# A four-layer graph network on one core: own terms two blocks ahead, a held bank of sums, later scatters and more buffers in layer 1

## The chip, the cores and the metric

The kernel runs on one core of one Trainium2 chip. Its metric is the device time of one execution in microseconds (us). TensorE (PE) multiplies matrices, VectorE (DVE) and ScalarE (ACT) work elementwise, GpSimd (POOL) here issues indirect DMAs (gathers and scatters by a list of row numbers), and SyncE (SP) issues the plain DMAs. [...]

## The reference, cut to what matters

Four layers follow each other; each adds its result to `x` (2708 rows of 128 numbers) and normalises every row. `adj` is a 2708 x 2708 matrix with about 0.6% of its entries set.

```python
x = _layernorm(x + _L0_gnn_ref(x, adj), axis=-1)            # adj.T @ x, divided by the column sums
x = _layernorm(x + _L1_gnn_ref(x, adj, msg_w, ...), axis=-1)
x = _layernorm(x + _L2_gnn_ref(x, adj, W, ...), axis=-1)    # adj @ (x @ W), batch norm, leaky relu
x = _layernorm(x + _L3_gnn_ref(x, adj, w1, ...), axis=-1)   # attention over neighbours, 4 heads

# layer 1, which the change is about
s = node_feats @ msg_w[:, :D].T
d = node_feats @ msg_w[:, D:].T
messages = jax.nn.gelu(s[:, None, :] + d[None, :, :] + msg_b, approximate=False)
aggregated = jnp.einsum('ijd,ij->id', messages, adj)
combined = jnp.concatenate([node_feats, aggregated], axis=-1)
new_feats = combined @ upd_w.T + upd_b
h = jax.nn.gelu(new_feats, approximate=False) + node_feats
mu, var = jnp.mean(h, axis=-1, keepdims=True), jnp.var(h, axis=-1, keepdims=True)
return (h - mu) / jnp.sqrt(var + LN_EPS) * ln_w + ln_b
```

Only the nonzero entries of `adj` contribute to `aggregated`. So for each row `i` the kernel needs the row `d[j]` of each neighbour `j`, adds the row's own term `s[i]` (with the bias), takes the gelu and sums with the weights `adj[i, j]`.

## The kernel before, in words

Rows are handled in 22 blocks of 128 (the last has 20). During layer 0, while the rows of `adj` stream through nine buffers, VectorE finds the nonzero entries of each row (`extract`) and the rows are ranked by their number of neighbours, in two groups of 13 and 9 blocks. Rows are then scattered to memory in that order (`dx_dram` holds for each row its `d` and its `x`, `d_dram` holds `d` in the original order), so that the rows of one block have about equally many neighbours: `CAPS` gives the number of gathers of each block, from 30 to 8, 368 in all.

Layer 1 goes over the blocks in the order `TURNS`; one pass of that loop is called a turn here. In a turn:

- `own_row` (L821) loads the next block's `d` and `x` on SP into `x_s` (three buffers).
- `messages` takes the one bank of the PSUM pool `own_ps`. It transposes the block's `x` (L832, TensorE), copies it out (L833, ScalarE), multiplies by the message weights and adds the bias (L834, L835), which leaves `s` in that bank. VectorE adds `s` to the block's own `d` (L849), ScalarE takes the gelu (L850). Then for each chunk of up to 8 neighbours POOL issues one gather per neighbour into a `msg` tile (L245; five tiles), VectorE adds `s` to all of them (L858), ScalarE takes the gelu (L861), and VectorE multiplies each by its weight and accumulates into one of two sums in the same bank (L844, L846), the last two into `parts`.
- In some turns `spread` prepares index lists of layer 3: lists loaded by SP (L580) are multiplied by a mask on VectorE (L601), multiplied on TensorE into free columns of the same bank (L607) and copied out (L614, L615).
- One or two other blocks of `adj` are transposed beside this (`transposed`, L931 on TensorE, L936 on ScalarE) and stored to `at_dram` by SP (L938); nine blocks are still searched by `extract`.
- `update` takes the one bank of `tail_ps`: it adds and transposes `parts` (L872), copies (L879), multiplies (L881 to L883), takes the gelu (L888), adds the residual (L889), normalises twice on VectorE (`x_n`, L319), scatters the result to `x2_dram` on POOL (L253), transposes it (L899, L901) and multiplies it by layer 2's weights (L903), and ScalarE puts the product into `xw` (L904).
- From the twelfth turn on `layer2` gathers whole rows of the transposed matrix (one indirect DMA each) and adds 22 products per block into six PSUM banks (L957).

The order of instructions on each engine is not the order of the source in this part. The pools record dependences, and a scheduler fixes one order for each engine ahead of time, by priority in the order of the source and by its own estimate of times[...]. Buffers of a pool are reused once the last reader is done. Layers 0 and 3 have orders written out by hand for some engines. After layer 1 the kernel loads `x2_dram`, does the batch norm of layer 2, and layer 3 gathers rows of 644 numbers 400 times.

Of the kernel before, what the change touches and what calls it, by code (L numbers as in the profile page):

```python
# [9 lines left out]
FP = mybir.dt.float32  # L10
AF = mybir.ActivationFunctionType
ALU = mybir.AluOpType
# [3 lines left out]
P = 128  # L16
N = 2708
D = 128
# [63 lines left out]
GOT = 9  # L82


@with_exitstack
def gnn_resnorm_kernel(
# [248 lines left out]
    with ExitStack() as layer:  # L335
# [6 lines left out]
        sums_ps = part.enter_context(tc.tile_pool(name="sums_ps", bufs=7, space=PSUM))  # L342
        hand.enter_context(tc.manual_schedule(engines={engine.DVE}))
# [26 lines left out]
        def weight(src, name):  # L370
            raw = small.tile([P, P], FP, name="raw_w")
            nc.sync.dma_start(raw, src)
            pt = own_ps.tile([P, 512], FP, name="pt_w", tag="own")
            nc.tensor.transpose(pt[:, 0:P], raw, ident)
            t = work.tile([P, P], FP, name=name)
            nc.scalar.copy(t, pt[:, 0:P])
            return t
# [101 lines left out]
        def ranking(g):  # L479
# [17 lines left out]
            key_row = work.tile([P, SPLIT, P], FP, name="key_row")  # L497
# [314 lines left out]
        msgs = layer.enter_context(tc.tile_pool(name="msgs", bufs=5))  # L812
# [5 lines left out]
        def own_row(b):  # L818
            n = BLOCKS[b][1]
            x_s = mine.tile([P, 2, D], FP, name="x_s", bufs=3)  # L820
            nc.sync.dma_start(  # L821
                x_s[0:n],
                dx_dram[b * P : b * P + n, :].rearrange("p (t d) -> p t d", t=2),
            )
            return x_s

        def messages(b, x_s, three):
            n, kk = BLOCKS[b][1], CAPS[b]
            po = own_ps.tile([P, 512], FP, name="own", tag="own")
            x_st, s_ps = mine.tile([P, P], FP, name="x_st"), po[:, P : 2 * P]  # L830
            acc = (po[:, 0:P], po[:, 3 * P : 4 * P])
            nc.tensor.transpose(po[:, 0:n], x_s[0:n, 1, :], ident[0:n, 0:n])  # L832
            nc.scalar.copy(x_st[:, 0:n], po[:, 0:n])  # L833
            nc.tensor.matmul(s_ps[0:n], lhsT=x_st[:, 0:n], rhs=ws_t, start=True, stop=False)  # L834
            nc.tensor.matmul(  # L835
                s_ps[0:n], lhsT=ones[0:1, 0:n], rhs=msgb[0:1, :], start=False, stop=True
            )
# [11 lines left out]
            nc.vector.tensor_tensor(mk, mk, s_ps[0:n], ALU.add)  # L849
            nc.scalar.activation(mk, mk, AF.Gelu)  # L850
            weigh(0, mk)
            for c0, c1 in chunks_of(kk):
                kc = c1 - c0
                msg = msgs.tile([P, 8, D], FP, name="msg")
                for k in range(kc):
# [3 lines left out]
                    mk, mk, s_ps[0:n].unsqueeze(1).to_broadcast((n, kc, D)), ALU.add  # L859
# [4 lines left out]
            for i, b3 in enumerate(three):  # L864
                spread(b3, po, 256 + 64 * i)
            return x_st, parts

        def update(b, x_s, x_st, parts):
# [16 lines left out]
            x_n = mine.tile([P, 1, D], FP, name="x_n")  # L885
# [12 lines left out]
            scatter(x2_dram, perm[0:n, b : b + 1], x_n[0:n, 0, :])  # L898
# [5 lines left out]
            nc.scalar.copy(xw[0:n, b, :], px)  # L904

        def transposed(b, rows, cleared=False):
# [10 lines left out]
            for j0 in range(0, NBLK, 4):  # L917
                count = min(4, NBLK - j0)
                pt = bank.tile([P, 4, P], FP, name="pt_a", tag="bank")
                at = small.tile([P, 4, P], FP, name="at_sb", bufs=3)  # L920
# [51 lines left out]
        ahead = own_row(0)  # L972
        left = list(range(SPLIT, NBLK))
        for i, b in enumerate(TURNS):
            if i == SPLIT - 2:
                sorted_lists(1)
            x_s, ahead = ahead, own_row(TURNS[i + 1]) if i + 1 < NBLK else None
# [6 lines left out]
            x_st, agg = messages(b, x_s, three)  # L984
            for _ in range(2 if i < 1 else 1):
                if left:
                    e = left.pop(0)
                    transposed(e, rows_of[e], True)
                    run(extract(e, rows_of[e]))
                    if e == NBLK - 3:  # L990
                        run(place(SPLIT, NBLK - 2, lists(SPLIT, NBLK - 2)))
                    if e == NBLK - 1:
                        run(place(NBLK - 2, NBLK, lists(NBLK - 2, NBLK)))
            update(b, x_s, x_st, agg)
# [7 lines left out]
            if i >= 11:  # L1002
                for k in range(2 * (i - 11), min(i, 2 * (i - 10))):
                    layer2(k)
        layer2(NBLK - 1)
# [1026 lines left out]
```

## Time and profile before

| | |
|---|---|
| time, median of 3 runs | 1605.33 us (1604.46 to 1609.47) |
| time of the profiled execution | 1957.99 us |
| its span, first to last instruction | 1956.3 us |
| mean granted TensorE clock in it | 0.668 |
| busy over the span: PE, DVE, ACT, POOL | 1248.6, 1173.2, 768.6, 896.4 us |
| first and last gather of messages | 229.8 and 1013.4 us |
| first and last scatter of layer 1's results | 352.4 and 1044.5 us |

The profile is one execution, recorded by hardware. A row of its groups gives a source line, an engine, an operation and its tiles (written tile, arrow, read tiles; numbers of buffers are left out, so `x_dram<-x_n` is the scatter into `x2_dram`), the count, then busy time and mean duration, then the engine's idle time just before these instructions and what ended it. "issue" is idle time in which the engine waited for nothing that the profile shows; "remote" is idle time ended by none of the core's engines or known transfers. A row of the timeline gives start, duration, the instruction, and in brackets the idle time before it. The profiled execution took 352.7 us more than the median of the timed ones, so its times are to be read with that in mind.

### The profile page before, as it was taken

The numbers are of one execution on the slowest core, as the hardware profiler recorded it, in microseconds if no ns is written. First come the engines' busy times: TensorE is split into PE (matmuls) and PEld (weight loads), VectorE is DVE, ScalarE is ACT, GpSimd is POOL, SyncE is SP. The second block draws the span as 40 slices with busy tenths as digits, with TensorE's granted clock in tenths as the row PEclk, the third lists the DMA queues.
The fourth block names the chain that finished last, engine by engine and source line by source line (L and its number), as shares of the span: only waits on it lengthen the run. The fifth ranks groups of instructions, "written<-read, shape, count | busy, mean of one in ns | idle before, by whom it ended". The sixth has DMA issues, their size and how long they took to land. (4 is left out here: it accounts for less than half of the span.)

```text
span 1956.3 us, 23628 instructions
## 1 busy us (share of the span) xinstructions
PE 1248.6 (64%) x5771; PEld 866.9 (44%) x5771; DVE 1173.2 (60%) x4900; ACT 768.6 (39%) x3134; POOL 896.4 (46%) x996
## 2 busy tenths in 40 slices
PE   7972414443345564556585647888798888877884
PEld 7972313333234453445465313445444444444444
DVE  8999536763353533343346626677678777676773
ACT  3475424542222311111111414455455555455543
POOL 1002655555544445444430454555565556555430
PEclk9985655555555576666677755677677777677675
DMA  8541547765444624332331474766475665756530
GB/s 288 228 160 41 170 94 195 202 169 145 125 90 117 173 96 96 109 132 88 141 110 37 153 222 130 190 189 194 140 206 178 173 178 153 189 159 191 153 109 7
DMA packets 164926, 289.61 MB, mean 148 GB/s; under 512 B 46850, under 2 KB 118752, under 8 KB 157679
## 3 DMA queue, kind: packets, MB, share of 16 engines
q0 software_dynamic: 60496, 190.76, 34.4%
q1 hardware_dynamic: 96739, 92.56, 15.6%
q10 hardware_dynamic: 7544, 4.69, 0.9%
q8 instruction: 48, 0.79, 0.2%
q14 instruction: 99, 0.81, 0.1%
HBM read 242.50 MB, written 45.35 MB: 147 GB/s over the span
## 5 line engine op out<-in xcount | busy, mean ns | idle before, releaser
L245 POOL DMA_INDIRECT g<-t_dram,idx x400 | 402.2, 1005 | 310.8 <-issue 169.2
L245 POOL DMA_INDIRECT msg<-d_dram,idx x368 | 348.7, 947 | 272.1 <-issue 225.7
L1324 ACT ACTIVATE sum_junk<-g 126x128 bf16<-126x128 f32 (+3 forms) x1024 | 302.6, 298 | 142.3 <-issue 60.8
L1293 PE MATMUL z<-x,copies 32*126 32x512 f32 (+3 forms) x800 | 220.3, 917 | 60.7 <-DVE g L1490 33.9
L957 PE MATMUL acc<-x_nat,at_rows 128*128 128x128 f32 (+2 forms) x968 | 168.8, 335 | 64.5 <-issue 52.6
L931 PE MATMUL pt_a<-ident,rows 128*128 128x128 f32 (+2 forms) x475 | 119.0, 408 | 131.5 <-ACT at_sb L936 106.9
L1490 DVE TENSOR_TENSOR g<-g,z 126x1536 f32<-126x1536 f32 (+3 forms) x100 | 175.1, 1751 | 40.1 <-remote 25.4
L1324 ACT ACTIVATION_READ_ACCUMULATOR sum_junk<-g 126x1 f32 (+3 forms) x1024 | 193.5, 189 | 0.0
L957 PEld LDWEIGHTS acc<-x_nat,at_rows 128*128 128x128 f32 (+2 forms) x968 | 151.2, 240 | 78.8 <-issue 67.5
L1298 PE MATMUL z<-g,ident 126*126 126x512 f32 (+3 forms) x200 | 168.5, 937 | 0.1
L1370 PE MATMUL po_s<-wm,g 126*128 126x24 f32 (+6 forms) x800 | 124.7, 310 | 59.7 <-DVE wm L1357 53.8
L931 PEld LDWEIGHTS pt_a<-ident,rows 128*128 128x128 f32 (+2 forms) x475 | 86.4, 212 | 154.8 <-ACT at_sb L936 120.9
L1370 PEld LDWEIGHTS po_s<-wm,g 126*128 126x128 f32 (+3 forms) x800 | 120.8, 237 | 75.1 <-DVE wm L1357 63.8
L1316 DVE SCALAR_TENSOR_TENSOR g<-g,a_ps 126x1536 f32<-126x1536 f32 (+6 forms) x100 | 151.1, 1511 | 0.0
L406 PE MATMUL acc<-x_nat,rows 128*128 128x129 f32 (+3 forms) x1012 | 128.5, 288 | 25.9 <-DMA rows<-in_adj_dram 15.1
L406 PEld LDWEIGHTS acc<-x_nat,rows 128*128 128x128 f32 (+2 forms) x1012 | 122.9, 197 | 31.1 <-DMA rows<-in_adj_dram 16.1
L846 DVE SCALAR_TENSOR_TENSOR own<-msg,ls,own 128x128 f32<-128x128 f32 (+1 forms) x302 | 106.5, 353 | 37.4 <-remote 13.5
L1293 PEld LDWEIGHTS z<-x,copies 32*126 32x126 f32 (+3 forms) x800 | 65.3, 250 | 97.9 <-issue 54.2
L1308 DVE SCALAR_TENSOR_TENSOR g<-z,a 126x128 f32<-126x128 f32 (+3 forms) x400 | 92.0, 287 | 19.4 <-DMA g<-t_dram,idx 9.4
L431 DVE FIND_INDEX8 ci<-cv,rows 128x8 uint32<-128x247 f32 (+2 forms) x242 | 101.6, 420 | 0.0
L436 DVE MAX8 cv<-rows 128x8 f32<-128x247 f32 (+2 forms) x242 | 98.0, 411 | 2.2 <-POOL rows L396 2.2
L1298 PEld LDWEIGHTS z<-g,ident 126*126 126x126 f32 (+3 forms) x200 | 41.7, 261 | 122.1 <-issue 109.1
(293 smaller groups left out, 2084.0 us busy)
## 6 DMA issues: line engine op xcount, KB each, us to landing
rows<-in_adj_dram SPq DMA_DIRECT2D x34, 1354.0 KB
at_dram<-at_sb SPq DMA_DIRECT2D x105, 256.0 KB
g<-t_dram,idx POOLq DMA_INDIRECT x400
msg<-d_dram,idx POOLq DMA_INDIRECT x368
t_dram<-t_row SPq DMA_DIRECT2D x21, 256.0 KB
x_s<-dx_dram SPq DMA_DIRECT2D x21, 128.0 KB
at_dram<-at_sb SPq DMA_DIRECT2D x21, 64.0 KB
d_dram<-dx SPq DMA_DIRECT2D x5, 256.0 KB
```

Of the source, the lines that this page charges most:

```text
L245: nc.gpsimd.indirect_dma_start(out=dst, out_offset=None, in_=table[0:N, :], in_offset=bass.IndirectOffsetOnAxis(ap=index, axis=0),)
L406: nc.tensor.matmul(accs0[k][0:m, c0 : c0 + f1 - f0], lhsT=rows[0:n, j0 : j0 + m], rhs=x_nat[0:n, b, f0:f1], start=k not in started, stop=( ...
L431: nc.vector.max_index(out=ci[0:n, at], in_max=cv[0:n, at], in_values=rows[0:n, c0 : c0 + cw])
L846: nc.vector.scalar_tensor_tensor(to, m, v, last, ALU.mult, ALU.add)
L931: nc.tensor.transpose(pt[0:m, j, 0:n], rows[0:n, c0 : c0 + m], ident[0:n, 0:n])
L957: nc.tensor.matmul(accs2[ib // 4][0:m, (ib % 4) * D : (ib % 4 + 1) * D], lhsT=at[0:n, i0 : i0 + m], rhs=xw[0:n, b, :], start=(k == 0 and i ...
L1293: nc.tensor.matmul(z3[0:e, r, :] if r < 3 else z1[0:e], lhsT=copies[g][rows, j, :], rhs=own[b][1][rows, :], start=True, stop=r < 3, skip_g ...
L1298: nc.tensor.matmul(z1[0:e], lhsT=ident[0:e, 0:e], rhs=g4[0:e, 3, 0:HD], start=False, stop=True, skip_group_check=True,)
L1316: nc.vector.scalar_tensor_tensor(z, z, 0.0, a_ps[0:e].unsqueeze(1).to_broadcast((e, count, HD)), ALU.max, ALU.mult)
L1324: nc.scalar.activation(junk[0:e], g4[0:e, r, hd * D : (hd + 1) * D], AF.Identity, accum_out=sc[0:e, r, hd : hd + 1],)
L1370: nc.tensor.matmul(po[:, p0 * HEADS : (p0 + g) * HEADS], lhsT=g4s[i][0:e, r, HD : HD + D], rhs=wm[0:e, 4 * i + r, :, :], start=True, stop= ...
L1490: nc.vector.tensor_tensor(z, z, z3[0:e], ALU.add)
```

## The change

Four things change in layer 1, and two tiles move to another pool.

1. **Own terms.** A new function `own_terms` makes the transposed `x` and `s` for a block; `s` is copied to SBUF. It uses the bank of `tail_ps` (same tag as the update's tile) and is called for the first two blocks before the loop and then in turn `i` for the block of turn `i + 2`, ahead of `update`. `own_row` is called three turns ahead instead of one. The adds in `messages` read `s` from SBUF.
2. **Sums.** One bank, `sums1`, is taken once before the loop and holds the two running sums in all turns; `spread` alternates between two sets of columns of it.
3. **Results.** `update` appends `x_n` to a list; `put_results` scatters what is in the list after the next turn's `messages`, and once after the loop.
4. **Buffers.** `msg` 5 to 6 tiles, `x_s` 3 to 4, `x_st` 2 to 3 and a new `s` with 3, `x_n` 2 to 3, the transposed tiles `at_sb` 3 to 5.
5. `raw_w` and `key_row` come from a pool `head`, which is given back at the end of layer 0.

```diff
+MSGS = 6
...
+        head = part.enter_context(tc.tile_pool(name="head", bufs=1))
...
-            raw = small.tile([P, P], FP, name="raw_w")
+            raw = head.tile([P, P], FP, name="raw_w", bufs=2)
...
-            key_row = work.tile([P, SPLIT, P], FP, name="key_row")
+            key_row = head.tile([P, SPLIT, P], FP, name="key_row")
...
-        msgs = layer.enter_context(tc.tile_pool(name="msgs", bufs=5))
+        msgs = layer.enter_context(tc.tile_pool(name="msgs", bufs=MSGS))
...
-            x_s = mine.tile([P, 2, D], FP, name="x_s", bufs=3)
+            x_s = mine.tile([P, 2, D], FP, name="x_s", bufs=4)
...
-        def messages(b, x_s, three):
+        def own_terms(b, x_s):
+
+            n = BLOCKS[b][1]
+            tp = tail_ps.tile([P, 512], FP, name="terms", tag="tail")
+            x_st = mine.tile([P, P], FP, name="x_st", bufs=3)
+            s = mine.tile([P, D], FP, name="s", bufs=3)
+            nc.tensor.transpose(tp[:, 0:n], x_s[0:n, 1, :], ident[0:n, 0:n])
+            nc.scalar.copy(x_st[:, 0:n], tp[:, 0:n])
+            pn = tp[0:n, P : 2 * P]
+            nc.tensor.matmul(pn, lhsT=x_st[:, 0:n], rhs=ws_t, start=True, stop=False)
+            nc.tensor.matmul(pn, lhsT=ones[0:1, 0:n], rhs=msgb[0:1, :], start=False, stop=True)
+            nc.scalar.copy(s[0:n], pn)
+            return x_s, x_st, s
+
+        def messages(b, x_s, s, three, spreads):
             n, kk = BLOCKS[b][1], CAPS[b]
-            po = own_ps.tile([P, 512], FP, name="own", tag="own")
-            x_st, s_ps = mine.tile([P, P], FP, name="x_st"), po[:, P : 2 * P]
-            acc = (po[:, 0:P], po[:, 3 * P : 4 * P])
-            nc.tensor.transpose(po[:, 0:n], x_s[0:n, 1, :], ident[0:n, 0:n])
-            nc.scalar.copy(x_st[:, 0:n], po[:, 0:n])
-            nc.tensor.matmul(s_ps[0:n], lhsT=x_st[:, 0:n], rhs=ws_t, start=True, stop=False)
-            nc.tensor.matmul(
-                s_ps[0:n], lhsT=ones[0:1, 0:n], rhs=msgb[0:1, :], start=False, stop=True
-            )
+            acc = (sums1[:, 0:P], sums1[:, 3 * P : 4 * P])
...
-            nc.vector.tensor_tensor(mk, mk, s_ps[0:n], ALU.add)
+            nc.vector.tensor_tensor(mk, mk, s[0:n], ALU.add)
...
-                    mk, mk, s_ps[0:n].unsqueeze(1).to_broadcast((n, kc, D)), ALU.add
+                    mk, mk, s[0:n].unsqueeze(1).to_broadcast((n, kc, D)), ALU.add
...
-                spread(b3, po, 256 + 64 * i)
-            return x_st, parts
+                spread(b3, sums1, P + 128 * (spreads % 2) + 64 * i)
+            return parts
...
-            x_n = mine.tile([P, 1, D], FP, name="x_n")
+            x_n = mine.tile([P, 1, D], FP, name="x_n", bufs=3)
...
-            scatter(x2_dram, perm[0:n, b : b + 1], x_n[0:n, 0, :])
+            results.append((b, x_n))
...
+        results = []
+
+        def put_results():
+            while results:
+                b, x_n = results.pop(0)
+                n = BLOCKS[b][1]
+                scatter(x2_dram, perm[0:n, b : b + 1], x_n[0:n, 0, :])
...
-                at = small.tile([P, 4, P], FP, name="at_sb", bufs=3)
+                at = small.tile([P, 4, P], FP, name="at_sb", bufs=5)
...
-        ahead = own_row(0)
+        sums1 = own_ps.tile([P, 512], FP, name="sums1", tag="own")
+        rows1 = [own_row(b) for b in TURNS[:3]]
+        terms = [own_terms(b, rows1.pop(0)) for b in TURNS[:2]]
...
-            x_s, ahead = ahead, own_row(TURNS[i + 1]) if i + 1 < NBLK else None
+            x_s, x_st, s = terms.pop(0)
+            if i + 3 < NBLK:
+                rows1.append(own_row(TURNS[i + 3]))
...
-            x_st, agg = messages(b, x_s, three)
+            agg = messages(b, x_s, s, three, i)
+            put_results()
...
+            if rows1:
+                terms.append(own_terms(TURNS[i + 2], rows1.pop(0)))
             update(b, x_s, x_st, agg)
...
+        put_results()
         layer2(NBLK - 1)
```

## The prediction

> **What bounds the kernel now.** I read four views in this order: the stretches, POOL's groups, VectorE's groups, then the timeline where engines stand still. Layer 1, with the re-read of the adjacency matrix and layer 2's sums beside it, runs from about 230 to 1050 us of the profiled span. First view: time, then each engine's busy time with its instruction count, granted clock, DMA share and GB/s.
>
> ```profile
> core 0: us, PE busy (x) PEld busy (x) DVE busy (x) ACT busy (x) POOL busy (x), PEclk, DMA share, GB/s
> 0.00:230.00 230.00, 150.01 (x1118) 139.42 (x1118) 205.54 (x1119) 121.02 (x190) 44.34 (x114) 0.83 0.50 172
> 230.00:1050.00 820.00, 402.23 (x1916) 329.54 (x1915) 362.67 (x1652) 213.92 (x472) 400.05 (x421) 0.60 0.46 129
> 1050.00:1130.00 80.00, 49.86 (x226) 32.36 (x225) 53.40 (x230) 30.67 (x87) 25.81 (x38) 0.81 0.37 118
> 1130.00:1956.00 826.00, 646.46 (x2516) 365.54 (x2516) 551.55 (x1901) 402.97 (x2386) 426.17 (x424) 0.68 0.58 163
> ```
>
> No engine is half busy in those 820 us. POOL issues 421 indirect DMAs there. The groups of POOL in that stretch (busy, mean ns, idle before and what ended it):
>
> ```profile
> L245 POOL DMA_INDIRECT msg<-d_dram,idx x368 | 348.7, 947 | 272.1 <-issue 225.7 <-ACT at_sb L936 30.3 <-ACT back L916 10.3
> L253 POOL DMA_INDIRECT x_dram<-x_n,perm x22 | 21.9, 996 | 134.1 <-DVE own L846 65.2 <-DVE x_n L319 51.7 <-DVE spread L601 14.2
> L245 POOL DMA_INDIRECT at_rows<-at_dram,perm x22 | 20.8, 946 | 6.7 <-issue 6.4 <-remote 0.3
> L253 POOL DMA_INDIRECT lists_dram<-lists,rank x9 | 8.9, 988 | 5.4 <-DMA lists_dram<-lists,rank 3.2 <-issue 2.1
> ```
>
> In the timeline consecutive gathers lie 1.25 us apart: 0.95 busy and 0.30 of gap. So 421 of them need 400 + 421 x 0.30 = 526 us without any wait. The other 820 - 526 = 294 us are waits: about 131 at scatters of results that wait for x_n, the rest for a free message buffer. VectorE's groups in the same stretch:
>
> ```profile
> L858 DVE TENSOR_TENSOR msg<-msg,own 128x896 f32<-128x896 f32 (+4 forms) x55 | 57.4, 1044 | 2.7 <-DVE rs_t L273 1.2 <-DVE rs_u L283 0.6
> ...
> L601 DVE TENSOR_TENSOR spread<-lists,of_row 128x126 f32<-128x126 f32 (+3 forms) x48 | 13.8, 291 | 104.3 <-remote 58.5 <-PE own L607 19.6 <-PE pt_a L931 13.1
> ...
> L889 DVE SCALAR_TENSOR_TENSOR new<-new,x_s 128x128 f32<-128x128 f32 (+1 forms) x22 | 6.4, 290 | 112.3 <-ACT new L888 95.2 <-issue 16.9
> L849 DVE TENSOR_TENSOR x_s<-x_s,own 128x128 f32<-128x128 f32 (+1 forms) x22 | 6.3, 286 | 49.5 <-PE own L835 36.8 <-remote 9.2 <-PE pt_a L931 3.5
> ```
>
> The first row is the one to weigh: the add that takes the gathered rows waited 2.7 us in all. In this execution the gathers were never late; VectorE was held by the update (L889), the own terms (L849) and the spreads. But the execution is not the timed one: its own time is 1957.99 us (span 1956.3), the median 1605.33, 352.7 less. The timeline of VectorE shows what is extra:
>
> ```profile
> 718.97 0.15 DVE L281 TENSOR_SCALAR rs_u<-rs_t 128x1 f32<-128x1 f32 x1 [0.61 <-issue]
> 721.07 0.16 DVE L283 TENSOR_TENSOR rs_u<-rs_u,rs_t 128x1 f32<-128x1 f32 x1 [1.95 <-remote]
> 722.46 0.16 DVE L285 SCALAR_TENSOR_TENSOR rs_y<-rs_u,rs_y 128x1 f32<-128x1 f32 x1 [1.23 <-DVE rs_u L283]
> 723.16 0.22 DVE L273 SCALAR_TENSOR_TENSOR rs_t<-rs_y,ln_var 128x1 f32<-128x1 f32 x1 [0.55 <-DVE rs_y L285]
> 724.56 0.15 DVE L289 TENSOR_SCALAR rs_t<-rs_t 128x1 f32<-128x1 f32 x1 [1.18 <-DVE rs_t L273]
> ```
>
> A chain of VectorE alone, 0.15 us a step, stops for 0.6 to 2 us between steps; from 768 to 806 us TensorE issues single matmuls 2 to 3 us apart in the same way, also with nothing to wait for. I take such stalls for the cost of recording. VectorE's waits that "issue" or "remote" ended sum to 5, 201, 6 and 104 us in the four stretches; sharing 352.7 us by 201/316 gives layer 1 some 224 us of it, so an estimated 596 us in a timed run. POOL's 526 us are then 88% of the stage, and 70 us of POOL waits are left. That is the bound I work with.
>
> [...]947 ns of POOL for each gather, whatever the other engines do. [...]here gathers queue behind a waiting scatter (13.67 us at 756 us). [...]
>
> **The change part by part**, with the built order of both kernels.
>
> Results scattered later. The same 22 scatters move behind gathers: the first 20 stood on average 16.2 gathers behind the last gather of the next block, now 29.2; the tightest, of the thirteenth turn, goes from 0 to 25, those of turns 16 to 18 from 7 or 8 to 16, 14 and 9. The last two stay at 0. One clean turn (809.2 to 828.1 us in the trace) has x_n 1.6 us after the turn's last add, so 5 us of lead or 4 gathers suffice once compute keeps up. Of the 70 us I leave 25 to the stretch behind the last gather (37 us in the profile, 1013 to 1050), which stays; the other 45 split as 131 : 163, so 20 us at scatters. I take 18 as removed. x_n's third buffer costs nothing while VectorE does not reach the fourth result before the first has gone.
>
> Message buffers, 5 to 6. Look-ahead goes from 5 x 6.7 = 33 gathers (42 us) to 40 (50 us). It cuts a stall by at most 8 us. Of the 25 us of buffer waits I take 8; bounds 0 and 25.
>
> Own terms ahead. Per block 1 transpose, 2 fp32 matmuls and a copy move; one copy of s is new (22 x 0.27 = 6 us of ScalarE, hidden: it is busy 214 of 820). VectorE's 49.5 us before L849 go, worth nothing on a POOL-bound stage except as slack. Reading s from SBUF: no gain, since 128x128 adds take 286 ns with PSUM (L849) and 282 without (L877). Two transposed copies and own-row buffers more: nothing by themselves. The terms now use the tail bank, between the last copy of one update and the first matmul of the next. Chain from the clean turn: x_n to the last copy 1.6 us, terms 2.5 (0.27 + 0.27 + 1.35 + 0.27 and hops), update to L889 2.8: 6.9 us, where VectorE has S, two adds and a multiply (2.8 us) ahead of L889. Uncovered: 4 us per turn. A clean turn takes 18.9 us, POOL needs (20 + 3) x 1.25 = 28.8 for that block: covered there. In the last four turns POOL needs 14 to 21 us and cover is gone: 4 x 1 us = 4 us lost.
>
> Own rows loaded three ahead. The 22 loads on SP stay, each now waiting for the previous turn's L889 instead of the one before that; behind them queue stores of transposed tiles and list loads for the spreads, 156.8 us of such SP waits today. List loads are issued two turns early. Bounds: 0 and 10 us lost through spreads; I take 0. One bank held: a spread's matmuls now stand among later sums in places (15 waits of VectorE for TensorE on the last sums, before none), under 1 us each and covered. Order of the neighbour search on VectorE: its work is the same and moves behind messages; 0. Memory for the key row freed early: 0.
>
> Sum: 18 + 8 - 4 = 22 us of the timed stage. Against the profiled execution it is 1957.99 - 22 or more, as its waits are larger; against the median, 1605.33 - 22 = 1583.
>
> **Rivals.** A: the timed run has cheaper gathers than 1.25 us, so the chain TensorE, ScalarE, VectorE is the bound, as in the trace. For: gathers never late there. Against: the stalls are the recording's. Then L849's 49.5 us and part of L889's 112 go: 60 to 75 us, 1530 to 1545. B: POOL is already dense, or its buffer waits were only the recording's: nothing moves, 1600 to 1610. C, slower: the tail bank. If every hop of the serial chain queues behind two layer-2 products (4 passes of 0.176 us, that is 165.8 us over 944 records of L957; five gaps: 3.5 us), the chain is 10.4 us and 7.6 uncovered, so a turn of 18.9 becomes some 25 us; POOL needs less than that in the last six turns (14 to 25), which lose 4 to 8 us each: about 35, less 15 of gain kept before: 1625. It decides once a turn's chain is longer than its gathers. For: before, the bank is already taken from 927.0 to 956.1 us of a 31.7 us turn. Against: most of that is x_n waiting in VectorE's order.
>
> **How the numbers follow.** Forecast 0.42 (own range 1565 to 1598), A 0.20, B 0.12, C 0.26. Faster 0.62, same 0.12, slower 0.26; 0.3%, or 5 us, is what this measurement can tell from no change. The range 1542 to 1625 leaves about a tenth outside at each end, in A and in C.
>
> **What would show it.** In the profile after: scatters of x_n without idle time of POOL before them (131 us now); L849's wait near zero; gathers dense at 1.25 us with fewer buffer waits; L889's wait no larger than 112. Wrong if L889 or the first matmul of the update waits more, with POOL idle for message buffers in the last turns (C), or if POOL's waits shrink and the time does not (B).

## The result: 2.8% slower, and where the profile shows it

The kernel after takes 1650.35 us (median of 4 runs, 1648.64 to 1656.08), the kernel before beside it 1607.40 us: a ratio of 1.0281, 95% interval 1.0252 to 1.0310. The forecast was 1583, its range ended at 1625.

Executions fall into two groups, whatever the kernel: before takes 1605 to 1614 us in the faster group and 1937 to 1952 us in the slower one (the expectations speak of two kinds of chip, but chip number 6 is on record with both, so that the chip decides is not shown).

The times above are from the faster group. The profile of before that the prediction read, 1957.99 us, is from the slower one, so its extra time was not a cost of recording: the profile of a copy of before with the same instruction lists (the first experiment) was recorded in the same way and took 1609.49 us, beside a median of 1609.96. VectorE's waits ended by "issue" or "remote" sum to 0.0 us in its layer 1, where the prediction summed 201. This copy is the profile of before in what follows.

The stretches of the copy of before in the faster group (time, busy time of each engine, TensorE clock, DMA share, GB/s); layer 1 is 223 to 830 us, batch norm up to 896, layer 3 behind:

```profile
core 0: us, PE busy (x) PEld busy (x) DVE busy (x) ACT busy (x) POOL busy (x), PEclk, DMA share, GB/s
223.00:830.00 607.00, 346.11 (x1886) 289.85 (x1885) 354.34 (x1632) 213.41 (x469) 402.26 (x423) 0.67 0.62 174
830.00:896.00 66.00, 43.53 (x224) 31.04 (x224) 52.16 (x223) 28.17 (x82) 24.10 (x37) 0.82 0.38 118
896.00:1607.00 711.00, 619.32 (x2541) 351.23 (x2539) 550.09 (x1909) 400.97 (x2392) 426.60 (x426) 0.72 0.70 192
```

The same stretches of after:

```profile
223.00:869.00 646.00, 349.19 (x1882) 295.67 (x1880) 335.33 (x1630) 215.84 (x488) 410.65 (x423) 0.65 0.56 163
869.00:935.00 66.00, 43.55 (x229) 30.46 (x228) 52.48 (x225) 28.83 (x84) 24.66 (x38) 0.84 0.40 124
935.00:1648.00 713.00, 613.45 (x2534) 348.63 (x2533) 550.45 (x1906) 400.88 (x2391) 425.77 (x425) 0.73 0.68 191
```

Layer 1 goes from 607 to 646 us, all else stays within 2 us. With 423 gaps of 0.30 us POOL is taken for 402 + 127 = 529 of the 607 us before and 538 of the 646 after; its waits grow from 78 to 108 us. POOL's groups in layer 1 (busy, mean ns | idle before), first of the copy of before:

```profile
L245 POOL DMA_INDIRECT msg<-d_dram,idx x368 | 348.8, 948 | 136.2 <-issue 107.0 <-ACT at_sb L937 13.3 <-DMA msg<-d_dram,idx 6.7
L253 POOL DMA_INDIRECT x_dram<-x_n,perm x22 | 21.9, 997 | 55.3 <-DVE x_n L319 33.6 <-DVE own L847 16.4 <-issue 3.1
...
L253 POOL DMA_INDIRECT lists_dram<-lists,rank x9 | 8.9, 985 | 6.2 <-DMA lists_dram<-lists,rank 2.8 <-DVE own L847 1.6 <-issue 1.5
```

then of after:

```profile
L247 POOL DMA_INDIRECT msg<-d_dram,idx x368 | 358.4, 974 | 120.8 <-issue 100.4 <-DMA msg<-d_dram,idx 10.3 <-ACT x_st L837 2.2
L255 POOL DMA_INDIRECT x_dram<-x_n,perm x22 | 21.9, 995 | 82.0 <-DVE x_n L321 46.8 <-DVE spread L604 19.9 <-DVE sums L855 12.0
...
L255 POOL DMA_INDIRECT lists_dram<-lists,rank x9 | 8.8, 973 | 25.6 <-DVE rs_t L275 10.7 <-DVE ln_var L293 7.4 <-DMA lists_dram<-lists,rank 4.4
```

Four numbers move: waits at the scatters of results 55.3 to 82.0 (+26.7), waits at the scatters of layer 3's lists 6.2 to 25.6 (+19.4), the gathers themselves 348.8 to 358.4 (+9.6), waits before gathers 136.2 to 120.8 (-15.4). They sum to 40.3 us; the two spans differ by 40.9, the medians by 43. (Each gather has at least 0.30 us of idle time before it, 110 us for 368 of them, in both profiles.)

VectorE's groups say the same from its side. The copy of before (add of messages; update's first add after the gelu; own add):

```profile
L859 DVE TENSOR_TENSOR msg<-msg,own 128x896 f32<-128x896 f32 (+4 forms) x55 | 57.4, 1044 | 15.8 <-DMA msg<-d_dram,idx 14.9 <-DVE ln_var L306 0.2
L890 DVE SCALAR_TENSOR_TENSOR new<-new,x_s 128x128 f32<-128x128 f32 (+1 forms) x22 | 6.4, 291 | 63.5 <-ACT new L889 63.5
L850 DVE TENSOR_TENSOR x_s<-x_s,own 128x128 f32<-128x128 f32 (+1 forms) x22 | 6.3, 286 | 21.8 <-PE own L836 21.7
```

and after:

```profile
L867 DVE TENSOR_TENSOR msg<-msg,s 128x896 f32<-128x896 f32 (+4 forms) x55 | 57.7, 1050 | 139.8 <-DMA msg<-d_dram,idx 121.2 <-issue 18.4
...
L858 DVE TENSOR_TENSOR x_s<-x_s,s 128x128 f32<-128x128 f32 (+1 forms) x22 | 6.4, 290 | 30.3 <-ACT s L841 30.3
L898 DVE SCALAR_TENSOR_TENSOR new<-new,x_s 128x128 f32<-128x128 f32 (+1 forms) x22 | 6.4, 289 | 43.8 <-ACT new L897 43.7
```

VectorE now waits 139.8 us before it adds to gathered rows (121.2 of them ended by the rows landing), 15.8 before, while POOL waits for VectorE. Each waits for the other in turn. One such turn in the timeline of after, VectorE first (start, duration, instruction, idle before):

```profile
697.22 0.96 DVE L867 TENSOR_TENSOR msg<-msg,s 128x768 f32<-128x768 f32 x1 [3.48 <-DMA msg<-d_dram,idx]
698.09 0.21 DVE L275 SCALAR_TENSOR_TENSOR rs_t<-rs_y,ln_var 128x1 f32<-128x1 f32 x1
...
700.13 0.15 DVE L291 TENSOR_SCALAR rs_t<-rs_t 128x1 f32<-128x1 f32 x1
705.24 0.96 DVE L867 TENSOR_TENSOR msg<-msg,s 128x768 f32<-128x768 f32 x1 [4.96 <-DMA msg<-d_dram,idx]
706.11 0.15 DVE L293 TENSOR_TENSOR ln_var<-rs_y,rs_t 128x1 f32<-128x1 f32 x1
...
711.98 0.34 DVE L321 TENSOR_SCALAR x_n<-new,sums,ln_var 128x128 f32<-128x128 f32 x1
```

and POOL in the same microseconds:

```profile
702.16 0.94 POOL L247 DMA_INDIRECT msg<-d_dram,idx  x1 [0.30 <-issue]
...
704.65 0.94 POOL L247 DMA_INDIRECT at_rows<-at_dram,perm  x1 [0.30 <-issue]
712.60 1.00 POOL L255 DMA_INDIRECT x_dram<-x_n,perm  x1 [7.01 <-DVE spread L604]
713.91 0.97 POOL L247 DMA_INDIRECT msg<-d_dram,idx  x1 [0.30 <-issue]
```

The rsqrt steps of one block's normalisation (L275 to L293) are threaded between the message adds of the next block. At 700.13 they stop: the next instruction of VectorE is an add whose rows land at 705.24. Only then does the chain go on, through a second normalisation threaded between the sums of those rows, to x_n at 711.98, and POOL, which came to that scatter at 705.6, stands 7 us. The gathers of the block after next start only at 713.91. The last releaser named is a spread, but x_n is ready at 712.32.

The built order is the order of each engine's instructions in the program as it was built. In the records above both engines keep to theirs: VectorE's chain stands 5.0 us behind that add, the next gather behind a scatter that waits 7.0 us. Counted in the built order, x_n of a block stood behind the adds of 12.9 gathers beyond its own block on average before, and 27.3 after. What matters at its scatter is the lead, the number of gathers that POOL issues between the last one that x_n needs and the scatter: from the thirteenth turn on 15, 16, 14, 13, 8, 7, 11, 5, 6, 0 before and 5, 2, 0, 0, 0, 1, 0, 0, 0, 0 after. The scatters of turns 14 to 19 wait 5.4, 7.0, 5.4, 3.6, 7.5 and 5.9 us there; in the copy of before all but two of turns 12 to 19 wait 0.3 (the others 1.6 and 0.8). The copy of before waits elsewhere: 48 of its 55.3 us stand at the eleventh scatter (16.9) and the last three (31.1; 32.7 in after).

### The profile page after: what moved, and what is told of

Same layout as the page of the kernel before. It is cut to its first block, busy times and chain, and to the rows that moved or that the text cites. A ratio compares the mean times of both kernels' runs of the same rounds, so it can differ in the third digit from the quotient of the medians.

```text
span 1648.7 us, 23658 instructions
## 1 busy us (share of the span) xinstructions
PE 1160.0 (70%) x5771; PEld 818.3 (50%) x5771; DVE 1147.3 (70%) x4900; ACT 768.3 (47%) x3156; POOL 904.3 (55%) x996
## 5 line engine op out<-in xcount | busy, mean ns | idle before, releaser
L247 POOL DMA_INDIRECT msg<-d_dram,idx x368 | 358.4, 974 | 120.8 <-issue 100.4
L1318 PE MATMUL z<-x,copies 32*126 32x512 f32 (+3 forms) x800 | 208.9, 875 | 23.0 <-DVE g L1515 21.5
L974 PE MATMUL acc<-x_nat,at_rows 128*128 128x128 f32 (+2 forms) x968 | 156.0, 318 | 85.7 <-DMA at_rows<-at_dram,perm 75.6
L948 PE MATMUL pt_a<-ident,rows 128*128 128x128 f32 (+2 forms) x475 | 102.8, 375 | 145.0 <-ACT at_sb L953 132.0
L974 PEld LDWEIGHTS acc<-x_nat,at_rows 128*128 128x128 f32 (+2 forms) x968 | 138.8, 223 | 96.3 <-DMA at_rows<-at_dram,perm 78.7
L1323 PE MATMUL z<-g,ident 126*126 126x512 f32 (+3 forms) x200 | 162.5, 906 | 10.3 <-DMA g<-t_dram,idx 10.2
L867 DVE TENSOR_TENSOR msg<-msg,s 128x896 f32<-128x896 f32 (+4 forms) x55 | 57.7, 1050 | 139.8 <-DMA msg<-d_dram,idx 121.2
L1395 PE MATMUL po_s<-wm,g 126*128 126x24 f32 (+6 forms) x800 | 114.9, 296 | 31.0 <-DVE wm L1382 29.1
L1395 PEld LDWEIGHTS po_s<-wm,g 126*128 126x128 f32 (+3 forms) x800 | 111.3, 220 | 46.7 <-DVE wm L1382 41.1
L870 ACT ACTIVATE msg<-msg 128x896 f32<-128x896 f32 (+4 forms) x55 | 50.1, 915 | 169.8 <-DVE msg L867 149.9
L855 DVE SCALAR_TENSOR_TENSOR sums<-msg,ls,sums 128x128 f32<-128x128 f32 (+1 forms) x302 | 105.1, 348 | 0.9 <-ACT msg L870 0.2
L1333 DVE SCALAR_TENSOR_TENSOR g<-z,a 126x128 f32<-126x128 f32 (+3 forms) x400 | 91.8, 285 | 12.8 <-PE z L1323 12.1
```

Of the source, the lines that this page charges most:

```text
L247: nc.gpsimd.indirect_dma_start(out=dst, out_offset=None, in_=table[0:N, :], in_offset=bass.IndirectOffsetOnAxis(ap=index, axis=0),)
L855: nc.vector.scalar_tensor_tensor(to, m, v, last, ALU.mult, ALU.add)
L948: nc.tensor.transpose(pt[0:m, j, 0:n], rows[0:n, c0 : c0 + m], ident[0:n, 0:n])
L974: nc.tensor.matmul(accs2[ib // 4][0:m, (ib % 4) * D : (ib % 4 + 1) * D], lhsT=at[0:n, i0 : i0 + m], rhs=xw[0:n, b, :], start=(k == 0 and i ...
L1318: nc.tensor.matmul(z3[0:e, r, :] if r < 3 else z1[0:e], lhsT=copies[g][rows, j, :], rhs=own[b][1][rows, :], start=True, stop=r < 3, skip_g ...
L1323: nc.tensor.matmul(z1[0:e], lhsT=ident[0:e, 0:e], rhs=g4[0:e, 3, 0:HD], start=False, stop=True, skip_group_check=True,)
```

## The experiments

All theories are named in the expectations: D, VectorE's order just shown; C, the serial chain through the tail bank (the slower rival of the prediction); S, the later search and list loads. In those texts the "turns 13 to 18" of the search-first kernel and the "turns 12, 14 and 16" of the one with s from SBUF count from zero; they are turns 14 to 19 and turns 13, 15 and 17 here.

Two parts can be judged without a run. With the scatter put back into `update`, or with `sums1` taken anew in each turn, the instruction lists of all five engines are those of after, instruction for instruction. So "results later" and "one bank held" are in the source only; what moved the scatters was the scheduler, by what else changed: by the prediction's own count, more buffers alone move them from 16.2 to 27.1 gathers behind.

**Copy of before** (only the pool `head`; the instruction lists are those of before).

> Kernel before with only the move of raw_w and key_row to the pool head. The instruction lists of all five engines are the same as before. Every theory: 1607 us, within 0.3%. It is run for its profile: before's profiled execution took 350 us more than its timed runs; this one should show layer 1 at about 600 us (before's 1607 less the 1002 us that the profile of after shows outside layer 1), with GpSimd (POOL) waiting some 60 us there, against 108 us in the kernel after (82 at the scatters of x_n, 26 at those of lists).

1609.96 us, ratio 1.0003 (0.9981 to 1.0024). Layer 1 is 607 us and POOL waits 78 us in it.

**Own terms alone** (after, with msg 5, at_sb 3 and x_n 2 buffers and the scatter in `update`).

> Kernel before plus own terms two blocks ahead and the held bank alone: msg 5, at_sb 3, x_n 2 buffers, scatter inside update. In the built order x_n still needs 23 gathers beyond its block's last on average (before 13, after 27), with 0 to 5 gathers between that and its scatter from the twelfth turn on, as in after. D: at least as slow as after, 1640 to 1670, since the buffers that help are missing. C: the same chain, 1630 to 1650. If the loss came from the more buffers (stores of transposed tiles running ahead on SP): 1607.

1651.66 us, 1.0254 (1.0213 to 1.0296). The own terms, with what comes with them (`s` in SBUF, own rows loaded three ahead), make the whole loss.

```profile
L247 POOL DMA_INDIRECT msg<-d_dram,idx x368 | 358.5, 974 | 139.8 <-issue 108.6 <-ACT at_sb L953 13.6 <-DMA msg<-d_dram,idx 4.6
L255 POOL DMA_INDIRECT x_dram<-x_n,perm x22 | 23.0, 1048 | 76.8 <-DVE x_n L321 47.7 <-DVE spread L604 16.9 <-DVE sums L855 8.4
```

**Own terms behind update**

```diff
-            if rows1:
-                terms.append(own_terms(TURNS[i + 2], rows1.pop(0)))
             update(b, x_s, x_st, agg)
+            if rows1:
+                terms.append(own_terms(TURNS[i + 2], rows1.pop(0)))
```

> Kernel after with own_terms called after update instead of before it in each turn. In the built order x_n needs one block beyond its own (15 gathers on average, before 13), its scatter stands 8 to 40 gathers behind that up to the turn before the last but one; the search still ends after 157 gathers and the lists scatters stand after 168 to 199, as in after. D: the waits at x_n scatters fall from 82 to about 30, 1595 to 1615. C: the chain of tail bank is broken up too (terms behind the update's last copy, not ahead of its first matmul), about 1610. S: unchanged search and list loads, 1640 to 1650.

1615.41 us, 1.0032 (1.0013 to 1.0051): 2.5 of the 2.8% are gone. POOL's groups, and the own add of VectorE:

```profile
L247 POOL DMA_INDIRECT msg<-d_dram,idx x368 | 360.8, 980 | 117.7 <-issue 97.8 <-DMA msg<-d_dram,idx 4.7 <-PE pt_a L948 3.6
L255 POOL DMA_INDIRECT x_dram<-x_n,perm x22 | 21.9, 996 | 46.2 <-DVE x_n L321 28.4 <-DVE wrong L621 12.3 <-issue 3.7
...
L255 POOL DMA_INDIRECT lists_dram<-lists,rank x9 | 9.0, 995 | 21.7 <-DVE rs_t L275 12.0 <-DVE rs_t L291 6.3 <-issue 1.8
...
L858 DVE TENSOR_TENSOR x_s<-x_s,s 128x128 f32<-128x128 f32 (+1 forms) x22 | 6.4, 293 | 95.5 <-ACT s L841 95.5
```

Against after, the waits at results fall by 35.8 us, those at lists by 3.9, the gathers stay slow. x_n now stands behind the adds of 15.4 gathers beyond its block, and the leads of turns 14 to 19 are 18, 17, 16, 14, 8 and 12. VectorE waits 65 us more for `s` than in after (95.5 against 30.3), and the kernel is some 35 us faster. S, which expected 1640 to 1650, falls as the main cause. D and C both expected about this time; they are told apart below.

**A fence in VectorE's order**. After `results.append`, with the next block's `s`:

```diff
+            if s_next is not None:
+                n = min(n, n_next)
+                nc.vector.scalar_tensor_tensor(
+                    s_next[0:n, 0:1], x_n[0:n, 0, 0:1], 0.0, s_next[0:n, 0:1],
+                    ALU.mult, ALU.add,
+                )
```

In one turn, where the next block has 20 rows, this also cuts the rest of `update` to 20 rows and so leaves 108 rows of one product for layer 2 out.

> Kernel after plus one 128x1 VectorE instruction per turn: after x_n of a block it rewrites column 0 of the next block's s as s + 0 * x_n, so that the adds of the next block's messages must come behind the normalisation in VectorE's order. In the built order x_n then needs no gather beyond its own block's last (in after: 27 more on average), and its scatter stands 25 to 46 gathers behind that one (in after: 0 to 5 from the thirteenth turn on). Theory D (VectorE's order: x_n queues behind adds that wait for gathers that are issued only after its scatter): POOL's 82 us at the x_n scatters fall to about 20, the time to 1570 to 1600. Theory C (the serial chain through the tail bank): the terms still stand between two updates in that bank, so 1640 or more. Theory S (the later neighbour search and list loads on SP): the search ends after 72 gathers here instead of 157, so S also expects a gain, but of the 26 us at the lists scatters only, 1620 to 1630, with the x_n waits left.

1639.78 us, 1.0175 (1.0129 to 1.0220), not the 1570 to 1600 that D was made to expect; C had expected 1640 or more.

```profile
L247 POOL DMA_INDIRECT msg<-d_dram,idx x368 | 357.8, 972 | 148.9 <-issue 120.7 <-DMA msg<-d_dram,idx 5.7 <-ACT at_sb L959 4.5
L255 POOL DMA_INDIRECT x_dram<-x_n,perm x22 | 23.6, 1071 | 51.8 <-DVE s L910 26.6 <-DVE x_n L321 17.9 <-DVE sums L855 2.8
```

The scatters of turns 14 to 19 wait 0.3 us each, as D said; 35 of the 51.8 us are the last two (17.3 and 17.9). But now VectorE ends each block before it begins the next, its waits in the update (L898) are 67.1 us up to 835 us against 29.0 in after, and POOL's waits before gathers go from 120.8 to 148.9, perhaps because message tiles come free later, which these rows do not show. C's mechanism is not seen in this profile: before the update's instructions TensorE waits for x_n (75.3 us), for the sums (15.6) and for two copies of the update itself (12.1 and 7.3), and before the terms it waits 5.8 us for the bank. So both too much and too little of the next block ahead of x_n cost time: some of it covers the update's hops, and more than the scatter's lead allows starves POOL.

**Own terms one block ahead**, behind update (`TURNS[:1]`, `TURNS[i + 1]`): the fence's order without a fence, and no terms in the tail bank between messages and update.

> Kernel after with own terms made one block ahead and behind update. Built order: x_n needs no gather beyond its own block's last, its scatters stand 25 to 46 gathers behind that, as with the fence. Here no terms stand in the tail bank between messages and update. If the fenced kernel was slow because VectorE finishes each block before it begins the next (waits for TensorE and ScalarE are then uncovered, and message buffers come free late): the same, 1630 to 1645. If it was slow because of the tail bank (C): 1605 to 1615.

Measured in the slower group only: 1969.73 us, 1.0120 (1.0047 to 1.0193) of before there, where after is at 0.9963 (below). So finishing block by block costs there too, with the tail bank's chain broken up. That, too, speaks against C for the fenced kernel; the numbers expected for the faster group stay untested.

**Search first**: after, with the leftover blocks' `transposed` and `extract` moved ahead of `messages` in the turn.

> Kernel after with the nine leftover blocks' transposition and neighbour search put ahead of messages in the source of a turn instead of behind. In the built order the scatters of layer 3's lists stand behind 149 to 186 gathers (after: 172 to 199, before: 142 to 179), and the scatters of x_n in turns 13 to 18 stand 14, 9, 7, 5, 7 and 4 gathers behind the last gather that x_n needs (after: 2, 0, 0, 0, 1, 0); x_n still needs 27 gathers beyond its own. Theory D with a need of about 4 gathers (5 us): the 35 us of waits of those turns go; the lists' 23 us go to about 5: 1590 to 1610. If the lists alone count: 1630. Theory C (tail bank): that chain is as in after, 1645 to 1655.

> The kernel after with the search put ahead of messages, once more. On the first kind of chip (before about 1607): D 0.990 to 1.000 of before, as the 35 us of scatter waits of turns 13 to 18 and some 18 us of the lists' waits go; the lists alone 1.013; C 1.025 to 1.03. On the second kind: 0.98 again, and then it is to be compared with the kernel after in the same call.

> The kernel after with the search put ahead of messages. On a chip where before takes about 1607 us: D with a need of about 4 gathers 0.990 to 1.003 of before (the 35 us of scatter waits of turns 13 to 18 and about 18 us of the lists' waits gone, the 10 us of slower gathers kept); the lists alone 1.013; C 1.025 to 1.03. On a chip where before takes about 1937: 0.98 again.

The first two are from the slower group: 0.9819 (0.9736 to 0.9901) and 0.9827 (0.9772 to 0.9882), a gain of 1.8% over before. The third, in the faster group: 1628.78 us, 1.0099 (1.0072 to 1.0126).

```profile
L247 POOL DMA_INDIRECT msg<-d_dram,idx x368 | 362.5, 985 | 121.2 <-issue 100.7 <-DMA msg<-d_dram,idx 5.7 <-DMA at_rows<-at_dram,perm 4.1
...
L255 POOL DMA_INDIRECT x_dram<-x_n,perm x22 | 22.1, 1002 | 67.0 <-DVE x_n L321 47.4 <-DVE seg L539 12.2 <-DVE spread L604 3.0
L255 POOL DMA_INDIRECT lists_dram<-lists,rank x9 | 9.2, 1025 | 12.0 <-DVE rs_t L291 7.1 <-DMA lists_dram<-lists,rank 3.4 <-issue 1.2
```

The lists' waits fall from 25.6 to 12.0. The scatters of turns 14 to 19 wait 0.3, 0.3, 3.0, 4.8, 1.6 and 3.2 us, 13 instead of 35, with 14, 9, 7, 5, 7 and 4 gathers between; so a lead of 4 to 7 is not enough in this kernel. It is no fixed number: with own terms behind update a lead of 8 left a wait of 6.0 us, and with s from SBUF leads of 6 left none. A new wait of 12.2 us appears at an earlier scatter. C, with its chain as in after, expected 1.025 or more; D had expected 0.990 to 1.003, the lists alone 1.013, and the time lies between.

**Buffers alone**: before with the pool `head`, msg 6, at_sb 5.

> Kernel before with the buffers alone: pool head, msg 6, at_sb 5. Built order: x_n needs 14 gathers beyond its own block's last, as before; the scatters stand 21 to 36 gathers behind that (before 5 to 28); the last four stand behind all gathers. D: the 17 us wait at one scatter in the middle (10 gathers behind) and 10 to 15 us of waits for message buffers go, the 31 us at the end stay: 1575 to 1590. If POOL was dense already: 1600 to 1610.

> Kernel before with the buffers alone (pool head, msg 6, at_sb 5). On the first kind of chip: 0.98 to 0.99 of before, if the 17 us wait at the eleventh turn's scatter and 10 us of buffer waits go there; 1.00 if POOL was dense. On the second kind: 1.00 to 1.005 again.

> Kernel before with the buffers alone (pool head, msg 6, at_sb 5). On a chip where before takes about 1607 us: 0.98 to 0.99 of before, if the 17 us wait at the eleventh turn's scatter and 10 us of buffer waits go there; 1.00 if POOL was dense. On the other: 1.00 to 1.005 again.

In the slower group 1.0051 (1.0017 to 1.0085) and 1.0009 (0.9980 to 1.0038); in the faster one 1598.94 us, 0.9926 (0.9902 to 0.9950), the one version found that beats both kernels there.

```profile
L245 POOL DMA_INDIRECT msg<-d_dram,idx x368 | 348.3, 946 | 127.3 <-issue 104.2 <-DMA msg<-d_dram,idx 6.3 <-ACT ln_junk L301 4.5
L253 POOL DMA_INDIRECT x_dram<-x_n,perm x22 | 21.9, 994 | 45.2 <-DVE x_n L319 38.8 <-issue 4.0 <-DVE own L847 0.9
```

That is less than the 0.98 to 0.99 expected. Only the last three scatters wait, 38.7 us; a wait of 16.9 us at the eleventh is gone. Here x_n's needs stay (13.9 gathers beyond its block), while the scatters stand 21 to 36 gathers behind them up to the nineteenth turn.

**s read from SBUF**: before, with one copy. It asks whether the place of `s` alone makes the gathers slow that begin during a message add.

```diff
+            s = mine.tile([P, D], FP, name="s")
+            nc.scalar.copy(s[0:n], s_ps[0:n])
...
-            nc.vector.tensor_tensor(mk, mk, s_ps[0:n], ALU.add)
+            nc.vector.tensor_tensor(mk, mk, s[0:n], ALU.add)
...
-                    mk, mk, s_ps[0:n].unsqueeze(1).to_broadcast((n, kc, D)), ALU.add
+                    mk, mk, s[0:n].unsqueeze(1).to_broadcast((n, kc, D)), ALU.add
```

> Kernel before with one edit: s is copied from its bank to SBUF by ScalarE, and the adds of messages read that copy. Nothing else of the change. [...]15 to 25 of the gathers take over 1.1 us, none in the kernel before; those that begin during an add take about 1.3 us on average against 0.94; together 8 to 13 us. Theory D: the adds no longer wait for the bank, so in the built order the scatters of turns 12, 14 and 16 stand 3, 1 and 1 gathers behind the last gather that x_n needs (before 15, 14, 8): about 10 us more of waits there. Both: 1620 to 1635; [...]D alone 1617; neither, 1607.

> Kernel before with s read from an SBUF copy. On the first kind of chip, where adds and gathers overlap more: gathers that begin during an add take about 1.3 us on average against 0.94, 8 to 13 us in all, and 10 us more of waits at the scatters of turns 12, 14 and 16: 1.008 to 1.015 of before. On the second kind: 1.00 to 1.005 again.

> Kernel before with s read from an SBUF copy, nothing else. On a chip where before takes about 1607 us: 15 to 30 gathers over 1.1 us, all of them begun during an add of messages, 8 to 13 us of POOL in all (none in before); some 10 us more of waits at the scatters of turns 12, 14 and 16, which stand 3, 1 and 1 gathers behind the last gather that x_n needs: 1.008 to 1.015 of before. [...]

> Kernel before with s read from an SBUF copy, nothing else; its three runs so far fell on chips where before takes 1937 to 1952 us. Where before takes about 1607: 15 to 30 gathers over 1.1 us, all begun during an add of messages, 8 to 13 us in all, and some 10 us more of waits at the scatters of turns 12, 14 and 16: 1.008 to 1.015 of before[...].

Slower group: 1.0032 (0.9991 to 1.0073), 1.0037 (1.0004 to 1.0070) and 1.0155 (1.0110 to 1.0200), so differences under one per cent are not settled there. Faster group: 1618.08 us, 1.0019 (0.9992 to 1.0047). The time, expected at 1.008 to 1.015, hardly shows it; the records do:

```profile
L245 POOL DMA_INDIRECT msg<-d_dram,idx x368 | 359.1, 976 | 129.4 <-issue 99.5 <-ACT at_sb L938 7.0 <-DMA msg<-d_dram,idx 6.0
```

10.3 us more of POOL than the copy of before, of which 6.8 come back as fewer waits before gathers. 41 gathers and scatters begin while a message add runs; they take 1.26 us on average, 24 of them over 1.1 us, and none of the others in layer 1 does. In the copy of before 44 begin so, with a mean of 0.94 and none over 1.1. In after it is 28, with 1.31 and 18. One of them, in the timelines of after:

```profile
242.44 1.09 DVE L867 TENSOR_TENSOR msg<-msg,s 128x896 f32<-128x896 f32 x1 [9.44 <-DMA msg<-d_dram,idx]
```

```profile
241.56 0.94 POOL L247 DMA_INDIRECT msg<-d_dram,idx  x1 [0.31 <-issue]
242.81 1.54 POOL L247 DMA_INDIRECT msg<-d_dram,idx  x1 [0.30 <-issue]
```

The gather that began 0.37 us into the add took 0.60 us longer. The waits expected at three scatters came: those of turns 13, 15 and 17 wait 14.7, 1.0 and 2.8 us, 0.3 each in the copy of before, and that of turn 19 7.7. But the 16.9 us of the eleventh are gone, so that the sum at results hardly moves (56.5 against 55.3).

**After in the slower group**, unchanged.

> The kernel after, unchanged, beside the others of this call. The chip of the last call ran every kernel slower (before 1939 us against 1607), with TensorE and the hops between engines slower and POOL's gathers not. If this is the first kind of chip: ratio to before 1.025 to 1.031, as recorded. If it is the second kind: POOL is less of a bound there and theory D expects the order of VectorE to cost less, ratio 0.99 to 1.02.

1935.94 us against 1937.10, ratio 0.9963 (0.9918 to 1.0009): no loss there. POOL's groups in its layer 1, to be held against the rows of before in the prediction, from the same group:

```profile
L247 POOL DMA_INDIRECT msg<-d_dram,idx x368 | 359.4, 977 | 163.0 <-issue 116.3 <-ACT at_sb L953 20.2 <-ACT ln_junk L303 6.3
L255 POOL DMA_INDIRECT x_dram<-x_n,perm x22 | 21.9, 997 | 160.5 <-DVE sums L855 47.0 <-DVE x_n L321 43.2 <-DVE spread L604 26.9
...
L255 POOL DMA_INDIRECT lists_dram<-lists,rank x9 | 9.5, 1058 | 44.1 <-DMA lists_dram<-lists,rank 21.4 <-DVE rs_t L275 19.9 <-DVE lists L543 1.8
```

The costs are the same or more (results +26, lists +39, gathers +11), but waits before gathers fall by 109 us, from 272.1 to 163.0, where the faster group had only 15 to give. That tiles and x_s coming earlier are worth more there, since VectorE stands still more often (201 us against 0.0 above), would explain it; no experiment shows it. These are single executions, which differ by 27 us where the medians differ by 1; the ratio is the firmer number.

**Both mended**: own terms behind update and search first.

> Kernel after with own_terms behind update and the search ahead of messages. If the parts add up as POOL's idle time says: waits at the x_n scatters as with own_terms behind update (46 us with gaps), at the lists' as with the search first (12), message buffers 118, gathers 361: 10 us less of POOL than before, 0.994 of before on a chip where that takes about 1607 us. If they don't add up: 1.003 to 1.01. On the other kind of chip: 0.98 to 1.00.

> Kernel after with own_terms behind update and the search ahead of messages; its first run fell on a chip where before takes 1952 us (1.001 of before). Where before takes about 1607: 0.994 of before if the parts add up, 1.003 to 1.01 if they don't.

Slower group 1.0011 (0.9982 to 1.0040), faster group 1612.93 us, 1.0003 (0.9985 to 1.0021): level with before, neither the 0.994 expected nor 1.003. The waits at results were as expected (44.5 us), those at lists 19.3 instead of 12.

POOL's four numbers in layer 1 in the faster group, from the group rows of each kernel (one execution each), beside the ratio of the timed runs to before:

| kernel | gathers | before gathers | at results | at lists | sum, less before's | ratio |
|---|---|---|---|---|---|---|
| copy of before | 348.8 | 136.2 | 55.3 | 6.2 | 0 | 1.0003 |
| after | 358.4 | 120.8 | 82.0 | 25.6 | +40.3 | 1.0281 |
| own terms alone | 358.5 | 139.8 | 76.8 | 18.2 | +46.8 | 1.0254 |
| terms behind update | 360.8 | 117.7 | 46.2 | 21.7 | -0.1 | 1.0032 |
| fence | 357.8 | 148.9 | 51.8 | 12.5 | +24.5 | 1.0175 |
| search first | 362.5 | 121.2 | 67.0 | 12.0 | +16.2 | 1.0099 |
| s from SBUF | 359.1 | 129.4 | 56.5 | 9.5 | +8.0 | 1.0019 |
| both mended | 358.8 | 122.5 | 44.5 | 19.3 | -1.4 | 1.0003 |
| buffers alone | 348.3 | 127.3 | 45.2 | 12.4 | -13.3 | 0.9926 |

One per cent is 16 us: the sum gives each ratio within 6 us. POOL's time line is the stage's time, which is what the prediction had built on.

## Why the prediction was wrong, step by step

- **The bound.** "The cost of recording" was the wrong reading of the stalls: an execution of the faster group, recorded in the same way, has none of them in layer 1. The estimate made from it held all the same, because these stalls come near to the whole difference between the groups, whatever their cause (316 us of VectorE's waits in the one profile and 5 in the other, where the spans differ by 348): layer 1 at 596 us and 70 us of POOL waits left, measured 607 and 78.
- **Results scattered later: -18 predicted, +26.7 measured.** This is the step that failed. It counted the scatters' lead from the last gather of the next block, which is about where x_n stood in VectorE's order before, and found 16.2 to 29.2. It took x_n's own place in that order as given. The own terms had moved it: adds of two blocks became ready early for the scheduler, which put them ahead of the normalisation, and counted from what x_n then needs the lead is 0 to 2 in turns 14 to 20, where the prediction's count gives 9 to 20. The 20 us that it took for scatters ahead of the end stood almost all at one of them before, the eleventh (16.9 us); turns 12 to 19 had 2 us to win and lost 34. The need of 4 gathers was also low: leads of 4 to 7 left waits in the search-first kernel. And the later scatters were put down to the wrong edit, one that changes no instruction.
- **Own terms ahead: 4 us lost predicted, measured as the whole loss.** The 4 us were for the tail bank in the last turns; the wait before L849 was taken to go and to be worth nothing. It did not go (21.8 us in the copy of before, 30.3 in after, now for ScalarE's copy of `s`). What went is the dependence behind it. Before, the next block's `s` came into the bank of sums only once this block's sums were done, so at most the next block's adds stood ahead of x_n, on average those of 12.9 gathers, and none of the block after that; in after those of both blocks do in many turns. Nothing in the sum charged for its absence.
- **Order of the neighbour search: 0 predicted, 19.4 us measured at the lists' scatters.** The last index search stands behind the adds of 84 gathers before and of 157 now, the last lists are scattered behind 199 gathers instead of 179, and POOL comes to them before VectorE has: the waits end on VectorE, at rsqrt steps in the same queue. "Its work is the same" was true and not the point.
- **s from SBUF: "no gain", measured +9.6 us on POOL.** Only VectorE's own duration was compared (286 and 282 ns), not what the move does to POOL. With that one edit 24 gathers and scatters take over 1.1 us, all begun during a message add; in the copy of before and with the buffers alone none do. Why such an add slows them is not shown. So the 947 ns for each gather "whatever the other engines do" held for the kernel before, not for after (974 on average).
- **Buffers: -8, measured about right.** With the buffers alone, waits before gathers fall by 8.9 us (15.4 in after), and the time by 11 us in all (1610.16 to 1598.94, ratio 0.9926).
- **Rival C had the sign and the wrong mechanism.** It expected L889 to wait more and VectorE's update to be late because of the tail bank. That wait fell, 63.5 to 43.8 us (L898), and before the update's first matmul (L881) TensorE waits for that bank 2.1 us in all. The search-first kernel leaves the terms where they are in that bank and ends at 1.0099: most of the 2.8% goes without touching the chain.
- **Signs to look for.** "Scatter waits gone" and "L849 near zero" both came out false; gathers were dense, with no wait over 2 us from 228 to 464 us and fewer buffer waits, as said. Of the other rivals, A fell because a gather costs 1.25 us in the faster group's profiles too, B because POOL's waits did move.

Open remain what makes the slower group slow, and one wait of 6 to 17 us at a single scatter between the seventh and the thirteenth turn, in the faster group in every kernel but the one with buffers alone. The count of gathers does not explain it: the leads there are 10 to 35, and only with s from SBUF 3. In after VectorE waits for list loads there (2.5 us up to 569.3 and 3.3 us up to 575.4, while that scatter waits 8.3 us, up to 576.3).

## What to carry to other kernels

When a change lets work become ready earlier, look in each engine's built order at what is now put ahead of a producer that another engine's queue waits for; the lead of a consumer is to be counted from the last thing its producer stands behind, on all engines in turn. A wait that costs nothing can be a fence that keeps a good order. And price an operand's move by what it does to other engines too (here 9.6 us of POOL), not by the instruction's own time alone.

## What was not expected of the hardware

- The same kernel takes 1605 to 1614 us in some executions and 1937 to 1952 in others; layer 1 of before is 607 us in one and about 820 in the other, while a gather takes 0.95 us of POOL in both. A change can lose 2.8% in one and nothing in the other, and the search-first kernel is at 1.01 of before in one and at 0.98 in the other.
- Gathers and scatters that begin while a message add reads both operands from SBUF took 1.26 us on average with `s` from SBUF (41 of them, the longest 1.97) and 1.31 in after (28, the longest 1.95). The 44 that begin during these adds in the copy of before, where `s` is read from its PSUM bank, took 0.94.
